# Spreading token weights by transfers from DRAM, and adding the causal mask inside the row maxima, in a two-layer hybrid kernel

## The chip, the cores and the metric

The kernel runs on one core of a Trainium2 chip, in one launch. Its time is the device time of that core in microseconds (us): the median of three runs before the change is 1032.24 us (1031.15 to 1035.77). A profile is one further execution with the hardware's profiler on; its times are set against its own total. The engines are PE (TensorE, products), DVE (VectorE), ACT (ScalarE), POOL (GpSimd) and SP (SyncE), which here only issues transfers.

## What is computed

The input `x` is 4 sequences of 512 tokens with 128 channels. Six blocks follow, each added to `x`; the first two matter here. The first is causal softmax attention with 16 heads of 8 channels, computed blockwise with a running row maximum:

```python
scores = scale * jnp.einsum('bhtd,bhsd->bhts', Q, kb)
future = kv_pos[None, :] > q_pos[:, None]
scores = jnp.where(future[None, None], -jnp.inf, scores)
m_new = jnp.maximum(m, jnp.max(scores, axis=-1, keepdims=True))
```

The second is a mixture of 8 experts, two per token, and it is used twice (behind the softmax attention and behind the FAVOR attention). A token enters an expert multiplied by its routing weight:

```python
scores = jax.nn.softmax(logits.astype(jnp.float32), axis=-1)
top_vals, idx = jax.lax.top_k(scores, K)
xs = xt[:, None, :] * weights[:, :, None]
for e in range(E):
    mask = (idx == e).astype(x.dtype)
    h = jax.nn.silu(jnp.einsum('tkd,hd->tkh', xs, w1[e]) + b1[e])
    x2 = jnp.einsum('tkh,dh->tkd', h, w2[e]) + b2[e]
    x3 = jnp.einsum('tkd,hd->tkh', xs, w3[e]) + b3[e]
    y = y + jnp.sum(x2 * x3 * mask[:, :, None], axis=1)
z = jax.nn.silu(xt @ sw1.T) * (xt @ sw2.T) @ sw3.T
```

FAVOR attention, a gated linear attention, two quantized feed-forward blocks and a retention block make up the rest.

## The kernel before

**Stages.** `x` stays in SBUF as `X`. The work is done per sequence (512 tokens). `attention` (L409) goes first, as a software pipeline of 96 steps plus a tail of 8 steps and more; PE's order is written out there, the other engines' order is left to the framework. After it everything from the experts to the end is emitted by one planner, `Clock.steps` (L178). Each stage is a generator that names what it needs; the planner keeps its own estimate of when each engine is free, and of all that could go next it emits what could start first, with a priority `far` (the table `FAR`, L39) between equals. The numbers in `clock.later("dve", 0.7, ...)` and `clock.pe(0.34)` are those estimates in us. PE, ACT, DVE and POOL then run exactly in the order in which the planner emitted; SP's order is left to the framework.

**Attention's maxima.** Step n works on a group of four heads, a part of the query chunks and two of the heads. `maxima` (L464) makes the scores of a query chunk of 128 rows against all keys up to its diagonal (128, 256, 384 or 512 columns) in a bank of PSUM. The diagonal block must be masked: `late` (L475) adds a matrix of 0 and -1e30 with one product per chunk and head, identity `identb` times `lateb`, both in bf16, into the same bank (256 products in all). `keep` (L480) then takes the row maximum with `tensor_reduce` on DVE (L484) straight from the bank into a column of `tops`. Eight steps later `weights` (L496) forms the exponentials: ACT reads the bank (L509), POOL sets the future to zero (L511). All banks come from one set of eight, so a bank that DVE or ACT has not read yet keeps PE waiting.

**Experts.** There are 8 rounds q (4 sequences, twice) of 8 experts. `route` (L659) finds the weights of the two chosen experts per token (DVE, then POOL), in `parts` (L692) written as three bf16 parts whose sum is exact (`split`, L627: three casts and two subtractions on POOL). `by_expert` (L701) transposes them on PE to `wT`, one row per expert and part. `scaled` (L720) spreads one expert's row over all 128 channels with a product of `wT` with a selecting matrix `sel` (24 rows, bf16) into a bank, and DVE multiplies the bank with the tokens `xnT` into `xe` (L725):

```python
ps = bank()
self.mm(ps, k["sel"][:, e * P:(e + 1) * P], wT[q][:3 * E])
xe = self.new(more["sm"], [P, T], "xe")
return xe, lambda: tt(xe, xnT[q], ps, ALU.mult)
```

`first` (L727) multiplies `xe` with w1 and w3 (two f32 products, each recorded as two instructions of 512 columns), ACT applies tanh and biases (L735, L737), DVE finishes the silu (L736: `h` and `g`, both in SBUF); `second` (L739) multiplies with w2 and forms `y`, on DVE from the bank (L746) or, for odd experts of rounds 0 to 4, on ACT and POOL (L747, L748); POOL adds `y` to the sum (L749). `total` (L751) adds the shared expert, a term for tokens that did not choose an expert (`c8` times the other rows of `wT`) and the sum into a bank, and DVE adds it to `X`. The generator `moe` (L1154) runs them in a pipeline: `spread` two experts ahead of `first`, `second` two behind it.

**Transfers.** SP's queue loads the inputs at the start, further weights when attention frees their room, stores `X` in DRAM once per sequence as `kept` (L1208), and stores the output at the end (L1687).

Of the kernel before, what the change touches and what calls it, by code (L numbers as in the profile page):

```python
# [10 lines left out]
F32 = mybir.dt.float32  # L11
BF16 = mybir.dt.np(mybir.dt.bfloat16)
U32 = mybir.dt.uint32
# [17 lines left out]
UP = 1.0 + 2.0 ** -22  # L31
EXP, TANH, SILU = ("exp",), ("exp", "silu"), ("silu",)
EARLY = 2

# [4 lines left out]
FAR = {  # L39
    "moe": (34,),  # L40
    "shared": (589, 230, 101, 186, 338, 444, 196, 385),
    "total": (34, 334, 167, 440, 467, 482, 19, 193),
    "in": (0, 0, 100, 527, 450, 482, 45, 323),
    "inward": (364, 104, 384, 461),
    "favor": (378, 171, 133, 588),
    "gates": (135, 468, 451, 231),
    "keys": (237, 481, 541, 82),
    "gated": (377, 269, 540, 166),
    "first": (55, 466, 547, 542),
    "retention": (54, 134, 224, 459),  # L50
    "leveled": (326, 293, 76, 394),
    "second": (75, 76, 343, 438),
}
# [3 lines left out]
def _constants():  # L57
    f = np.float32
    c = {}
    c["ident"] = np.eye(P, dtype=f)  # L60
    r = np.arange(P)
    g, d = r // 32, r % 32
    of = d[:, None] // DH == np.arange(NG)[None, :]
    row = d[:, None] == DH * ((np.arange(NG) + 1) % NG)[None, :]
    c["rows"] = np.concatenate([of, row, of | row], axis=1)
    c["heads"] = r[:, None] // DH == np.arange(H)[None, :]
    c["own"] = np.tile(r[:, None] % 32 // DH == r[None, :] // M, (1, 2))
    c["first"] = np.tile(np.arange(E, 0, -1, dtype=f), (P, 1))
    c["two"] = (r[:, None] // DI == np.arange(2)[None, :]).astype(f)
    lev = np.zeros((P, 6, 64), f)  # L70
    for l in range(6):
        right = r[(r >> l) & 1 == 1]
        lev[:, l, :] = ((r[:, None] >> (l + 1)) == (right[None, :] >> (l + 1))) & ((r[:, None] >> l) & 1 == 0)
    c["lev"] = lev.reshape(P, -1)
    c["tri"] = r[:, None] <= r[None, :]

    lo, hi = f(np.log(1.0 - 0.999)), f(np.log(1.0 - 0.9))
    gam = (f(1.0) - np.exp(np.linspace(lo, hi, H, dtype=f)).astype(f)).astype(np.float64)
    hd, mid = gam[r // DH], r - P // 2
    c["qdec"] = hd[:, None] ** mid[None, :]  # L80
    c["kdec"] = hd[:, None] ** -mid[None, :]
    c["cdec"] = hd[:, None] ** P
    of = r[:, None] // DH == r[None, :] // DH
    c["same"] = of * c["cdec"]
    c["group"] = (d[:, None] // DH == np.arange(NG)[None, :])
    c["avg"] = of / DH
    c = {k: np.ascontiguousarray(v.astype(f)) for k, v in c.items()}

    c["lateb"] = np.where(r[None, :] > r[:, None], f(-1e30), f(0)).astype(BF16)

    c["sel"] = np.repeat(np.arange(3 * E)[:, None] % E == np.arange(E)[None, :], P, axis=1).astype(BF16)
    c["identb"] = np.eye(P, dtype=f).astype(BF16)
    return c
# [142 lines left out]
class Net:  # L236
# [172 lines left out]
    def attention(self, beside=None, ended=None):  # L409
# [12 lines left out]
        with ExitStack() as ctx:  # L422
# [3 lines left out]
            tops = [self.new(big, [P, J, P], f"tops{G}") for G in range(NG)]  # L426
            vs = [self.new(big, [P, J, H, 32], f"vpad{i}") for i in range(2)]
            for t in tops:
                nc.vector.memset(t, 0.0)
# [34 lines left out]
            def maxima(g, s, h):  # L464
# [6 lines left out]
                def score(i, n):  # L471
                    c, o = step[n]
                    self.mm(ps[i][:, o:o + (c + 1) * P], q[strips[i], chunks[c]], kk[strips[i], :(c + 1) * P], start=(n == 0), stop=False)

                def late():  # L475
                    for i in heads:
                        for n, (c, o) in enumerate(step):
                            self.mm(ps[i][:, o + c * P:o + (c + 1) * P], k["identb"], k["lateb"], start=False, stop=(n == len(step) - 1))

                def keep():  # L480
                    r = 8 * ((G + 1) % NG)
                    for i in heads:
                        for c, o in step:
                            nc.vector.tensor_reduce(top[:, c, 32 * i + r:32 * i + r + 1], ps[i][:, o:o + (c + 1) * P], AX.X, ALU.max)  # L484

                return [[lambda i=i, n=n: score(i, n) for n in range(len(step))] for i in heads], late, keep

# [8 lines left out]
            def weights(g, s, h):  # L496
# [16 lines left out]

                return [[lambda i=i, n=n: score(i, n) for n in range(len(step))] for i in heads], lambda: None, keep

# [58 lines left out]
            with self.tc.manual_schedule(engines={mybir.EngineType.PE}):  # L574
# [4 lines left out]
                while n < max(at):  # L579
# [7 lines left out]
                    for i in range(2):  # L587
                        for strip in range(2):
                            for todo, _, _ in now:
                                if i < len(todo[strip]):  # L590
                                    todo[strip][i]()
                    for _, late, _ in now:
                        late()
                    for _, _, keep in now:
                        keep()
# [6 lines left out]

    def experts(self, ctx):
        nc, k = self.nc, self.k
# [8 lines left out]
        def enlarge(ctx):  # L613

            for name, bufs in (("mid", 2), ("sm", 4)):
                more[name] = ctx.enter_context(self.tc.tile_pool(name="e_" + name, bufs=bufs))
# [4 lines left out]
        half, half3, twice2 = (self.new(big, [P, E], n) for n in ("half", "half3", "twice2"))  # L621
        bf16 = mybir.dt.bfloat16
        W8 = 32 + 3 * E
        c8 = big.tile([W8, P], bf16, tag="c8", name=self.nm("c8"))
        xn, xnT, wT, shares, sums, part = ({} for _ in range(6))

        def split(to, x):  # L627

            for i in range(3):
                nc.gpsimd.tensor_copy(to[..., i, :], x)  # L630
                if i < 2:
                    nc.gpsimd.tensor_tensor(x, x, to[..., i, :], ALU.subtract)

        def of_none():
# [11 lines left out]
            stt(none, none, -1.0, b3, ALU.mult, ALU.mult)  # L646
            parts = big.tile([P, W8], bf16, tag="c8p", name=self.nm("c8p"))
            nc.gpsimd.memset(parts[:, :32], 0.0)
            split(parts[:, 32:].rearrange("p (k e) -> p k e", e=E), none)
            ps = bank([W8, P], bf16)  # L650
            nc.tensor.transpose(ps, parts, k["identb"])
            nc.scalar.copy(c8, ps)
# [6 lines left out]
        def route(q):  # L659
# [32 lines left out]
            def parts():  # L692
                nc.gpsimd.tensor_tensor(s, s, c, ALU.mult)
                w = part[q] = rt.tile([P, J, W8], bf16, tag="part", name=self.nm("part"))
                v = w.rearrange("p j (k e) -> p j k e", e=E)
                nc.vector.tensor_scalar(v[:, :, 3:], c.unsqueeze(2).to_broadcast([P, J, 4, E]), -1.0, 1.0, ALU.mult, ALU.add)
                split(v, s)

            return less, lambda: nc.scalar.activation(s, s, AF.Exp), shared_out, again, parts

        def by_expert(q):  # L701

            ps = bank([W8, T], bf16)
            for j in range(J):
                nc.tensor.transpose(ps[:, chunks[j]], part[q][:, j], k["identb"])
            wT[q] = pre.tile([W8, T], bf16, tag="wT", name=self.nm("wT"))
            return lambda: nc.scalar.copy(wT[q], ps)

# [11 lines left out]
        def scaled(q, e):  # L720

            ps = bank()
            self.mm(ps, k["sel"][:, e * P:(e + 1) * P], wT[q][:3 * E])
            xe = self.new(more["sm"], [P, T], "xe")
            return xe, lambda: tt(xe, xnT[q], ps, ALU.mult)  # L725

# [177 lines left out]
    def front(self, out):  # L904
# [5 lines left out]
        with ExitStack() as ctx, ExitStack() as now, self.tc.tile_pool(name="kept", bufs=1, space=bass.MemoryType.DRAM) as dram:  # L910

            rooms = ("identb", "ws", "first", "we", "sel")
            self.room(tp(now, "w", 1), rooms)
            ex = self.experts(now)
            with ExitStack() as att:
                self.load(tp(att, "wa", 1), ("wa", "rows", "lateb"))
                right = tp(att, "qw", 1, side="right")
# [175 lines left out]
            with ExitStack() as over, self.banks():  # L1093
# [29 lines left out]
                def routed(q):  # L1123
# [16 lines left out]
                    yield [op, when("y", q - 3) if q > 2 else 0.0], "bank"  # L1140
                    known["in", q] = later("act", 0.6, pe(0.5), ex.by_expert(q), "bank")
                    yield known["in", q]
# [11 lines left out]
                def moe():  # L1154
# [4 lines left out]
                    def spread(n):  # L1159
                        q, e = all_[n]  # L1160
                        yield [when("in", q)], "bank"
                        x, do = ex.scaled(q, e)
                        xe[n] = x, later("dve", 0.7, pe(0.34), do, "bank")
                        if e == E - 1:
                            known["left", q] = clock.since

# [10 lines left out]

                    for n in range(-2, len(all_) + 2):
                        if n + 2 < len(all_):
                            yield from spread(n + 2)  # L1180
                        if 0 <= n < len(all_):
# [671 lines left out]
```

## Time and profile before

| What | Value |
|---|---|
| median of 3 runs | 1032.24 us |
| profiled execution, total | 1032.06 us |
| its span, first to last instruction | 1030.3 us |
| mean granted clock of PE | 0.94 |
| ACT, busy | 560.0 us (54%) |
| transfers, whole span | 9.82 MB, 10 GB/s |
| attention ends (its last addition to X) | about 243 us |
| last product of the experts | 643 us |

A row of a group reads: line, engine, operation, output and inputs by the program's names, partitions x elements, count, then busy time and mean ns of one, then the idle time of that engine ahead of them and what ended it. Almost every product has line 400, a helper, so products are told apart by their tiles. Products overlap, so what one costs PE is read from the timeline, from its start to the start of the next, and not from its own duration.

### The profile page before, as it was taken

To read this page: it belongs to the slowest core of one execution; us is meant where nothing else is said; L and a number is where in the kernel's file an instruction comes from. 1 tells how busy PE (TensorE), PEld (TensorE's weight loads), DVE (VectorE), ACT (ScalarE), POOL (GpSimd) and SP (SyncE) were. 2 spreads that over 40 slices of the span, in tenths; PEclk is the share of its full clock that TensorE was granted. 3 is DMA by queue.
4 is the path that set the end of the run, shared out by engine and by line. 5 is a ranking of instruction groups with operands and counts; after the bars stand their busy time and mean duration, and the time that the engine had idled before them with its cause. 6 is when DMAs were issued, how large, how long until landed. Compare 5 with 4: busy or idle time off the path is not lost.

```text
span 1030.3 us, 17949 instructions
## 1 busy us (share of the span) xinstructions
PE 890.4 (86%) x6624; PEld 541.1 (53%) x6624; DVE 734.2 (71%) x1808; ACT 560.0 (54%) x1076; POOL 448.3 (44%) x899
## 2 busy tenths in 40 slices
PE   5999999998999989998988989678798977778734
PEld 3545555554335555444534457446687765566523
DVE  5657777755776898978877755596685864977664
ACT  3556656564774665757476742384345555465422
POOL 2434544341674554555556424463224515343322
PEclk9989999999999999999999999898998997997867
DMA  4000001000000000000000000100000000000000
GB/s 158 2 2 2 2 16 41 2 1 22 0 1 1 1 1 1 2 0 2 11 1 11 1 1 11 32 1 1 1 1 2 1 1 2 1 12 1 12 10 14
DMA packets 8387, 9.82 MB, mean 10 GB/s; under 512 B 1740, under 2 KB 6860, under 8 KB 8036
## 3 DMA queue, kind: packets, MB, share of 16 engines
q1 hardware_dynamic: 8292, 8.60, 2.6%
q8 instruction: 54, 0.88, 0.3%
q14 instruction: 41, 0.34, 0.1%
HBM read 6.50 MB, written 2.10 MB: 8 GB/s over the span
## 4 chain that ended last, share of the span: by engine, by line
PE 53%; DVE 27%; POOL 8%; ACT 7%; issue 4%; DMA 1%; SPq 0%; DVEq 0%; ACTq 0%; POOLq 0%
PE bank L400 48%; DVE D L1015 2%; DVE arg L831 2%; PE bank L382 2%; DVE top L828 1%; DVE h L736 1%; DVE bn L330 1%; DVE D L1606 1%; DVE D L1605 1%; PE bank L1655 1%; DVE top L829 1%; POOL rnt L310 1%; PE bank L492 1%; POOL rstdbe1t L310 1%; DVE den L887 1%
## 5 line engine op out<-in xcount | busy, mean ns | idle before, releaser
L484 DVE TENSOR_REDUCE tops<-bank 128x1 f32<-128x128 f32 (+3 forms) x256 | 110.1, 485 | 55.3 <-PE bank L400 55.2
L400 PE MATMUL bank<-xe,we 128*128 128x512 f32 x256 | 127.6, 620 | 4.5 <-ACT x L737 2.9
L509 ACT ACTIVATE w<-bank 128x512 f32<-128x512 f32 (+1 forms) x192 | 90.5, 526 | 69.5 <-PE bank L400 65.8
L511 POOL TENSOR_SCALAR_AFFINE_SELECT w<-w 128x128 f32<-128x128 f32 x256 | 70.3, 297 | 116.6 <-ACT w L509 116.1
L400 PE MATMUL bank<-qm,kz 32*128 32x384 f32 (+3 forms) x512 | 101.9, 471 | 1.1 <-DVE tops L484 0.6
L400 PE MATMUL bank<-kz,q 32*128 32x512 f32 (+3 forms) x512 | 98.2, 476 | 0.0
L749 POOL TENSOR_TENSOR sum<-sum,y 128x512 f32<-128x512 f32 x56 | 76.7, 1369 | 43.9 <-DVE y L746 41.6
L736 DVE SCALAR_TENSOR_TENSOR h<-h,g 128x512 f32<-128x512 f32 x64 | 60.2, 941 | 21.2 <-ACT g L735 21.1
L400 PEld LDWEIGHTS bank<-xe,we 128*128 128x128 f32 x256 | 43.6, 190 | 49.2 <-issue 29.7
L400 PE MATMUL bank<-h,we 128*128 128x512 f32 x128 | 67.4, 610 | 2.1 <-DVE arg L831 2.1
L735 ACT ACTIVATE h<-bank,half 128x512 f32<-128x512 f32 x64 | 43.8, 684 | 31.6 <-PE bank L400 31.3
L403 DVE TENSOR_TENSOR X<-X,bank 128x512 f32<-128x512 f32 x32 | 21.9, 685 | 50.8 <-PE bank L400 33.0
L400 PE MATMUL bank<-xs,wg 128*128 128x512 f32 x96 | 52.9, 657 | 5.0 <-DVE R L1308 3.3
L400 PEld LDWEIGHTS bank<-kz,q 32*128 32x128 f32 x512 | 38.2, 189 | 32.1 <-issue 11.6
L400 PEld LDWEIGHTS bank<-qm,kz 32*128 32x128 f32 x512 | 47.4, 185 | 13.1 <-DVE tops L484 2.3
L400 PE MATMUL bank<-w,vpad 128*32 128x256 f32 (+3 forms) x512 | 49.0, 449 | 1.8 <-DVE ru L675 1.1
L725 DVE TENSOR_TENSOR xe<-xnT,bank 128x512 f32<-128x512 f32 x64 | 43.2, 678 | 9.9 <-PE bank L400 9.9
L1741 POOL TENSOR_SCALAR_AFFINE_SELECT rw<-rw 128x1024 f32<-128x1024 f32 x32 | 35.4, 1122 | 31.8 <-ACT rw L1740 31.8
L737 ACT ACTIVATE x<-bank,half 128x512 f32<-128x512 f32 x64 | 44.0, 688 | 0.0
L735 ACT ACTIVATE g<-bank,ws 128x512 f32<-128x512 f32 x64 | 43.7, 682 | 0.0
L1740 ACT COPY rw<-bank 128x512 f32<-128x512 f32 x64 | 32.9, 596 | 14.4 <-PE bank L400 14.3
L382 PE MATMUL bank<-ident,xn 128*128 128x128 f32 x80 | 17.5, 314 | 24.9 <-ACT xn L342 19.0
(426 smaller groups left out, 2163.2 us busy)
## 6 DMA issues: line engine op xcount, KB each, us to landing
we<-in_we_dram SPq DMA_DIRECT2D x1, 1536.0 KB, 6.9
wg<-in_wg_dram SPq DMA_DIRECT2D x1, 1280.0 KB, 6.1
X<-in_x_dram SPq DMA_DIRECT2D x4, 256.0 KB, 4.4
kept<-X SPq DMA_DIRECT2D x4, 256.0 KB, 2.5
out_dram<-X SPq DMA_DIRECT2D x4, 256.0 KB, 2.3
wf<-in_wf_dram SPq DMA_DIRECT2D x1, 560.0 KB, 7.5
ws<-in_ws_dram SPq DMA_DIRECT2D x1, 400.0 KB, 4.6
wb<-in_wb_dram SPq DMA_DIRECT2D x1, 320.0 KB, 2.9
```

The source lines that it names most:

```text
L382: self.nc.tensor.transpose(ps[:, j * P:(j + 1) * P], xn[:, j, :], self.ident)
L400: self.nc.tensor.matmul(out, lhsT=lhsT, rhs=rhs, start=start, stop=stop)
L484: nc.vector.tensor_reduce(top[:, c, 32 * i + r:32 * i + r + 1], ps[i][:, o:o + (c + 1) * P], AX.X, ALU.max)
L509: nc.scalar.activation(w[:, :end], ps[i][:, :end], AF.Exp, scale=scale)
L511: nc.gpsimd.affine_select(out=w[:, o:o + P], in_=w[:, o:o + P], pattern=[[1, P]], compare_op=ALU.is_ge, fill=0.0, base=0, channel_multipli ...
L725: return xe, lambda: tt(xe, xnT[q], ps, ALU.mult)
L735: return (h, x3, lambda: (act(h, ph, AF.Tanh, scale=0.5, bias=half[:, e:e + 1]), act(g, ph, AF.Identity, bias=b1[:, e:e + 1])), lambda: st ...
L736: lambda: stt(h, h, 1.0, g, ALU.add, ALU.mult),
L737: lambda: act(x3, p3, AF.Identity, scale=0.5, bias=half3[:, e:e + 1]))
L749: lambda: nc.gpsimd.tensor_tensor(sums[q], sums[q], y, ALU.add))
L1740: ops = [later("act", 0.6, t, lambda n=n, i=i: nc.scalar.copy(w[n][:, i, :], pp[2 * n + i]), "bank") for i in range(2)]
L1741: ended.append(later("pool", 1.15, ops, lambda flat=flat: nc.gpsimd.affine_select(out=flat, in_=flat, pattern=[[0, 2 * J], [1, P]], compar ...
```

## The change

1. **Mask.** `late` and its 256 products go, with `lateb` and `identb`. A constant `late` of 128 x 512 in f32 takes their place: zeros, and the triangle of -1e30 in the last 128 columns. `keep` uses one fused DVE operation that adds the last `e` columns of `late` (SBUF) to the scores (bank), writes the sum to a scratch tile `junk` and the maximum to the column of `tops`.
2. **Token weights.** The three bf16 parts and `sel` go; the weights stay f32 (one part of 8 columns). `by_expert` copies the transposed rows to SBUF and then stores 8 rows of 512 in DRAM (`rows_of[q]`). `scaled` reads one row back to all 128 partitions by a transfer (SP) into `xe`, out of five buffers of its own (two ahead and three more), and multiplies it in place with `xnT`: on DVE for odd experts, on POOL for even ones. It takes no bank. `c8`, the transposes and the products with them become f32.
3. **Planner.** The rows of a round count as ready 5.5 us after the copy; the scaling counts as 0.85 us on DVE or 1.4 us on POOL, 0.5 us after it is emitted. A round counts as left when its last scaling has been done, not when it is emitted. All priorities in `FAR` have other values.

```diff
-    "moe": (34,),
-    "shared": (589, 230, 101, 186, 338, 444, 196, 385),
-    "total": (34, 334, 167, 440, 467, 482, 19, 193),
+    "moe": (80,),
+    "shared": (394, 388, 591, 530, 598, 130, 157, 493),
+    "total": (127, 37, 531, 99, 92, 3, 562, 529),
...
+    late = np.zeros((P, T), f)
+    late[:, T - P:] = np.where(r[None, :] > r[:, None], f(-1e30), f(0))
...
-                def late():
-                    for i in heads:
-                        for n, (c, o) in enumerate(step):
-                            self.mm(ps[i][:, o + c * P:o + (c + 1) * P], k["identb"], k["lateb"], start=False, stop=(n == len(step) - 1))
...
-                            nc.vector.tensor_reduce(top[:, c, 32 * i + r:32 * i + r + 1], ps[i][:, o:o + (c + 1) * P], AX.X, ALU.max)
+                            e = (c + 1) * P
+                            nc.vector.tensor_tensor_reduce(
+                                out=junk[:, :e], in0=ps[i][:, o:o + e], in1=k["late"][:, T - e:], scale=1.0, scalar=-3e38,
+                                op0=ALU.add, op1=ALU.max, accum_out=top[:, c, 32 * i + r:32 * i + r + 1])
...
+            for name, bufs in (("mid", 2), ("sm", 4), ("xe", AHEAD + 3)):
...
+                nc.gpsimd.tensor_tensor(v[:, :, 0], s, c, ALU.mult)
+                nc.vector.tensor_scalar(v[:, :, 1:], c.unsqueeze(2).to_broadcast([P, J, 4, E]), -1.0, 1.0, ALU.mult, ALU.add)
...
+            def keep():
+                nc.scalar.copy(wT[q], ps)
+                nc.sync.dma_start(rows_of[q], wT[q][:E])
...
-            ps = bank()
-            self.mm(ps, k["sel"][:, e * P:(e + 1) * P], wT[q][:3 * E])
-            xe = self.new(more["sm"], [P, T], "xe")
-            return xe, lambda: tt(xe, xnT[q], ps, ALU.mult)
+            xe = self.new(more["xe"], [P, T], "xe")
+            nc.sync.dma_start(xe, rows_of[q][e, :].partition_broadcast(P))
+            return xe, lambda eng: eng.tensor_tensor(xe, xnT[q], xe, ALU.mult)
...
-                    known["in", q] = later("act", 0.6, pe(0.5), ex.by_expert(q), "bank")
+                    op = later("act", 0.6, pe(0.5), ex.by_expert(q), "bank")
+                    known["in", q] = later(f"rows{q}", 5.5, op)
...
-                        xe[n] = x, later("dve", 0.7, pe(0.34), do, "bank")
+                        if e % 2:
+                            xe[n] = x, later("dve", 0.85, clock.since + 0.5, lambda: do(nc.vector))
+                        else:
+                            xe[n] = x, later("pool", 1.4, clock.since + 0.5, lambda: do(nc.gpsimd))
                         if e == E - 1:
-                            known["left", q] = clock.since
+                            known["left", q] = xe[n][1]
```

## The prediction

> **What bounds the kernel now.** I read the page's engine rows first, then busy time by stretch, the chain of waits, the costliest groups, and PE's timeline where the change cuts.
>
> ```profile
> PE 890.4 (86%) x6624; PEld 541.1 (53%) x6624; DVE 734.2 (71%) x1808; ACT 560.0 (54%) x1076; POOL 448.3 (44%) x899
> 25.00:225.00 200.00, 195.64 (x1906) 103.12 (x1904) 142.26 (x393) 118.03 (x244) 84.69 (x319) 0.98 0.03 9
> 243.00:312.00 69.00, 68.71 (x186) 28.42 (x187) 51.98 (x103) 45.29 (x78) 39.21 (x48) 1.00 0.03 8
> 312.00:602.00 290.00, 264.92 (x1463) 137.31 (x1462) 228.76 (x469) 182.35 (x322) 151.59 (x285) 0.99 0.01 3
> 645.00:1030.00 385.00, 289.01 (x2546) 224.16 (x2545) 267.54 (x704) 183.08 (x371) 144.88 (x174) 0.86 0.02 6
> PE 53%; DVE 27%; POOL 8%; ACT 7%; issue 4%; DMA 1%; SPq 0%; DVEq 0%; ACTq 0%; POOLq 0%
> ```
>
> The first line is the page's, the next four are busy time by stretch (start:end, length, then PE, PEld, DVE, ACT, POOL, granted clock, DMA share, GB/s), the last is the chain. Attention fills the first stretch, the experts alone the second, the experts beside FAVOR and the first gates the third, gates, retention and FFN the last. PE is 98%, 100% and 91% busy in the three that the change touches and 75% in the one that it does not. So work taken off PE in the first three can show. In attention DVE is second, at 71%.
>
> **Part 1: the mask.** The 256 mask products go; the 256 reductions become reductions of a sum with a second operand.
>
> ```profile
> L400 PE MATMUL bank<-lateb,identb 128*128 128x128 bf16 x256 | 31.4, 226 | 0.0
> L484 DVE TENSOR_REDUCE tops<-bank 128x1 f32<-128x512 f32 x64 | 41.1, 685 | 7.7 <-PE bank L400 7.7
> L494 DVE SCALAR_TENSOR_TENSOR qm<-q,rows,bank 128x512 f32<-128x512 f32 x16 | 11.9, 743 | 1.0 <-PE bank L492 1.0
> L1015 DVE TENSOR_TENSOR_SCAN D<-run,D 128x512 f32<-128x512 f32 x16 | 20.5, 1338 | 1.4 <-ACT D L1010 1.4
> L725 DVE TENSOR_TENSOR xe<-xnT,bank 128x512 f32<-128x512 f32 x64 | 43.2, 678 | 9.9 <-PE bank L400 9.9
> 137.59 0.28 PE L400 MATMUL bank<-lateb,identb 128*128 128x128 bf16 x2
> 137.81 0.64 PE L400 MATMUL bank<-w,vpad 128*32 128x256 f32 x8
> ```
>
> Products overlap, so their 226 ns is no price. The timeline gives it: two start at 137.59 and the next work at 137.81. Over all of attention the median is 0.21 us for the 64 pairs (0.12 to 0.22) and 0.32 for the 32 fours (0.23 to 0.33): 64 x 0.19 + 32 x 0.29 in the mean = **21.5 us of PE**. In the chain between 25 and 245 us PE's lines hold some 86% (products 76.5%, the transposes of L492, L535, L382 and L1535 another 9%), so 18.5 us of it should be felt.
>
> The new DVE operation is not in this trace. From below: a plain sum with one operand in a bank and one in SBUF takes 678 ns, the reduction 685, so it may cost nothing more, and I see no reason for less since as many elements stream. From above: the scan, the only row that carries a result from element to element beside a second operand, takes 1338, that is 0.65 more for 512 elements and 0.41 for the mean width of 320. The nearest row is the three-operand operation out of a bank, 743: +0.06 us each. Then DVE has 142.3 + 243 x 0.06 = 157 us of work in a stretch that PE would leave at 200 - 20 = 180: 87%. That still lies beside PE, but it hands back banks later, for which PE already waits 10.3 us here (13 times, on the maxima), so I charge 2.5 us. The product's end no longer stands between the scores and the maxima, which helps and is in the 18.5. Part 1: **-16 us**, ends -21.5 and +42 (below). The scratch output that all 256 share is written by one engine in order and adds no wait across engines.
>
> The accumulator deserves a sentence of its own. The Trainium skill, "VectorE: DVE Perf Modes", section "Two Vector instructions with no wait between them", has it that an operation that also writes out its accumulator is two instructions, the main one and a read of the accumulator; no instruction here does that, so no run here shows it.
>
> **Part 2: the token weights.** 64 products (L723) go, 64 transfers of 256 KB come, and the scaling of even experts moves to POOL.
>
> ```profile
> 283.74 0.39 PE L400 MATMUL bank<-wT,sel 24*128 24x512 bf16 x1
> 284.06 1.98 PE L400 MATMUL bank<-xe,we 128*128 128x512 f32 x4
> L736 DVE SCALAR_TENSOR_TENSOR h<-h,g x64: 666/692/1747, 257.4 to 625.1; 128x512 f32<-128x512 f32 x64
> L725 DVE TENSOR_TENSOR xe<-xnT,bank x64: 671/678/689, 251.4 to 594.0; 128x512 f32<-128x512 f32 x64
> L749 POOL TENSOR_TENSOR sum<-sum,y 128x512 f32<-128x512 f32 x56 | 76.7, 1369 | 43.9 <-DVE y L746 41.6
> kept<-X SPq DMA_DIRECT2D x4, 256.0 KB, 2.5
> ```
>
> - **PE.** One product holds PE for 0.32 us (283.74 to 284.06), 64 of them 20 us: 22 in the second stretch, 42 in the third. Products and transposes that turn from bf16 to f32 give some back: 32 of `total`'s at 0.08 become like its f32 neighbours (0.12), 32 transposes go from 0.085 to 0.12, together +2.4. The second stretch is paid in full (22 x 0.31 = 6.9). Of the third's 13.1 I count 45%, PE's product share of the chain there (43.5%): 5.9. Net -10.4.
> - **DVE** loses 64 x 0.68 = 43 us and gets 32 operations with both operands in SBUF. The rows show what that means: with an operand in a bank the time is 671 to 689 ns, with both in SBUF (L736) 666 to 1747, mean 941, the long ones lying beside a POOL operation. 32 x 0.94 = 30, so DVE is 13 us lighter, less some 6 if L736 gets 0.1 longer beside a busier POOL.
> - **POOL** gets 32 x 1.37 = 44 and loses 24 casts (7.4) and 16 subtractions (4.6). In the second stretch: 39 + 10 x 1.37 - 3 = 50 of about 63 us, 79%. In steady state an expert of the first five rounds now has two POOL operations, 2.74 us, against PE's 3.09 - 0.31 = 2.78. It stays under, barely; that is the first thing to fail.
> - **Transfers.** 256 KB landed 2.3 to 4.4 us after issue; 16.8 MB over 350 us are 48 GB/s, where the first slice moved 158. Five buffers let a transfer start when the product three experts earlier has read its buffer, about 8 us ahead of need, so 2.5 to 4.4 us are covered by PE's own work; without that cover 64 x 2.5 us would be exposed. SP issues 0.45 us each, in one queue with the stores of `kept`: a store that waits would hold up what stands behind it. The two-hop way through DRAM (2.5 + 2.5 us, eight times) is ahead of need by a round, and in the first two rounds falls inside attention. The very first transfer needs room that attention frees around 242; the shared products cover 243 to 250, so I charge nothing, at most 3 us.
>
> Part 2: **-10 us**, ends -18 (all of PE's time) and +10 (POOL late in the first rounds, SP's queue blocked a few times).
>
> **Part 3: the order.** All priorities are new, so the planner emits another order from 243 us on. In the last stretch no work changes, and I see in the trace no reason for a sign. Its longest single waits (PE for POOL's L1612: 10.3 and 7.5 us) set the size: one such wait more or less, **0, within 12 us**.
>
> **Sum.** The profiled execution took 1032.06 us (span 1030.3), 0.2 below the median of 1032.24. 1032.1 - 16 - 10 = **1006 us**.
>
> **Rivals.**
> 1. *All of it is felt and the order is kind*: -21.5 - 17.7, up to 10 more from the order: 984 to 994. For it: PE has hardly a gap in two stretches. Against: in the third stretch DVE and ACT end many waits. 0.13.
> 2. *DVE becomes attention's bound.* If each maximum costs a small second instruction (the nearest, a reduction of 32 elements, has 187 ns) on top of 0.06, DVE has 142.3 + 243 x 0.25 = 203 us in what is now 200. Attention then gains nothing (+3), the experts keep -10: 1018 to 1028, middle 1025. By the page named above this is what would happen. 0.12.
> 3. *Slower: the fused maximum runs at the scan's rate.* 142.3 + 243 x 0.41 = 242 us for 200: +42 - 10 = 1064 (1048 to 1075). It decides from about 0.28 us more per maximum, where 142.3 + 243 x 0.28 = 210 eats both gains. For it: the scan is the only kin in the trace that carries a value. Against: the plain reductions carry a running maximum at 685 ns. 0.08.
> 4. *The gain is given back*: POOL or SP's queue late in the experts (+10 where I have -10) or a worse order at the end (+12): 1028 to 1044. 0.17.
> 5. *The forecast*, 994 to 1018: 0.50.
>
> About 0.5% (5 us) is what a measurement of this kernel can tell from no change. Faster by more: 0.50 + 0.13 + 0.10 of rival 2 = 0.73; within: 0.02 of rival 2 and 0.05 of rival 4 = 0.07; slower: 0.12 of rival 4 and 0.08 of rival 3 = 0.20. The range 985 to 1042 leaves out rival 3 and the edges.
>
> **What would show it.** Right: attention ends near 225 instead of 241, its DVE row for 512 elements stands at 0.69 to 0.80 us, PE stays above 95% there; the pure expert stretch runs at 2.8 us per expert. Wrong: a DVE row of 0.95 us or more, or a second small row beside it, with PE waiting for the maxima; POOL above 90% with products waiting for `xe`; transfers that land later than 5 us after issue; a last part (now 387 us, from the end of the experts at 643 to the end) that changes by more than 12 us.

## The result and the profile after

| Kernel | median us | runs | ratio to before, 95% |
|---|---|---|---|
| before (same chip) | 1031.70 | 4 | |
| after | 1019.11 (1017.53 to 1020.30) | 4 | 0.9876 [0.9860, 0.9892] |

The change makes the kernel 12.6 us faster, where the forecast was 26 and its range 985 to 1042. The profiled execution took 1018.07 us (span 1016.1). These lines answer to the ones of before: the engine row and the chain from the page, then busy time by stretch (the last one ends with the kernel at 1016; the experts still run in its first 22 us).

```profile
PE 871.8 (86%) x6336; PEld 542.2 (53%) x6336; DVE 750.2 (74%) x2032; ACT 558.2 (55%) x1076; POOL 490.0 (48%) x887
...
PE 49%; DVE 30%; POOL 10%; ACT 6%; issue 5%; DMA 0%; SPq 0%; DVEq 0%; ACTq 0%; POOLq 0%
```

```profile
25.00:225.00 200.00, 192.64 (x1683) 97.03 (x1683) 156.84 (x637) 120.00 (x250) 85.25 (x322) 0.95 0.03 9
243.00:312.00 69.00, 62.22 (x183) 29.64 (x183) 49.68 (x102) 43.93 (x78) 50.75 (x60) 0.95 0.26 80
312.00:602.00 290.00, 250.54 (x1363) 143.88 (x1362) 212.07 (x414) 165.84 (x297) 164.47 (x249) 0.90 0.13 39
645.00:1016.00 371.00, 295.15 (x2726) 229.54 (x2724) 280.21 (x726) 186.79 (x380) 153.40 (x179) 0.90 0.02 6
```

Two columns tell the story. PE has less to do, but in the second and third stretch it is no longer full (62 of 69 us where it was 68.7; 250.5 of 290 where it was 264.9), and its **granted clock** (the share of full speed that it was given), 0.98, 1.00 and 0.99 before, is 0.95, 0.95 and 0.90. DVE's busy time in attention is 156.8 against 142.3, the 157 that the forecast had. Attention (to the start of its last addition to X) ends at 238.1 instead of 242.3; the rest takes 778.0 instead of 788.0 us.

A sum over stretches of 5 us splits each span in three: PE's work as it would be at full clock, what the clock took (busy time x (1 - granted clock), an estimate, since the ends of products are modelled), and PE's idle time.

| Kernel | span | work | clock | idle |
|---|---|---|---|---|
| before | 1030.3 | 847 | 43 | 140 |
| after | 1016.1 | 810 | 62 | 144 |

The change took 37 us of work off PE, about what the forecast counted (21.5 + 20 - 2.4 = 39). 19 came back as a lower clock and 4 as waiting. The sum is good to some 10 us only: it gives 843 for the run with the new order alone (below), whose instructions are those of before, and 11 and 21 us less than before for two runs that leave out the same 256 products. These totals hide that the kernel's parts moved in opposite ways. The same sum by part (the experts' part goes to their last product, at 643 before and 667 after):

| Part | length, before and after | work | clock | idle |
|---|---|---|---|---|
| attention | 242.3, 238.1 | 222, 207 | 3, 11 | 17, 20 |
| experts' part | 400.9, 429.3 | 371, 353 | 3, 28 | 27, 48 |
| last part | 387.1, 348.7 | 254, 249 | 37, 23 | 96, 76 |

In the experts' part, where the token weights changed, 18 us of work went and 46 of clock and idle time came; the last part, whose code did not change, is 38 us shorter. The experiments ask where the waits come from, and what the new table does by itself.

### The profile page after: what moved, and what is told of

It reads as the page before. It is cut to its first block, busy times and chain, and to the rows that moved or that the text cites. A ratio compares the mean times of both kernels' runs of the same rounds, so it can differ in the third digit from the quotient of the medians.

```text
span 1016.1 us, 17875 instructions
## 1 busy us (share of the span) xinstructions
PE 871.8 (86%) x6336; PEld 542.2 (53%) x6336; DVE 750.2 (74%) x2032; ACT 558.2 (55%) x1076; POOL 490.0 (48%) x887
## 4 chain that ended last, share of the span: by engine, by line
PE 49%; DVE 30%; POOL 10%; ACT 6%; issue 5%; DMA 0%; SPq 0%; DVEq 0%; ACTq 0%; POOLq 0%
PE bank L399 44%; DVE junk L480 2%; PE bank L381 2%; DVE h L728 2%; DVE D L1007 2%; DVE bn L329 1%; DVE D L1602 1%; DVE den L879 1%; POOL sum L741 1%; DVE D L1601 1%; POOL D L1608 1%; POOL xe L717 1%; PE bank L490 1%; PE bank L533 1%; DVE X L402 1%
## 5 line engine op out<-in xcount | busy, mean ns | idle before, releaser
L480 DVE CUSTOM_DVE_ANT_0 junk<-bank,late 128x128 f32<-128x128 f32 (+3 forms) x256 | 125.2, 489 | 41.1 <-PE bank L399 20.2
L399 PE MATMUL bank<-xe,we 128*128 128x512 f32 x256 | 134.2, 651 | 13.6 <-POOL xe L717 11.6
L399 PE MATMUL bank<-qm,kz 32*128 32x256 f32 (+3 forms) x512 | 109.7, 484 | 0.8 <-DVE tops L480 0.7
L399 PE MATMUL bank<-kz,q 32*128 32x512 f32 (+3 forms) x512 | 104.8, 494 | 1.2 <-ACT kz L462 0.6
L399 PEld LDWEIGHTS bank<-xe,we 128*128 128x128 f32 x256 | 50.8, 208 | 74.6 <-issue 47.0
L399 PE MATMUL bank<-h,we 128*128 128x512 f32 x128 | 71.3, 642 | 2.4 <-DVE KD L1043 1.2
L399 PEld LDWEIGHTS bank<-kz,q 32*128 32x128 f32 x512 | 43.1, 196 | 36.6 <-DVE tops L480 15.3
L399 PEld LDWEIGHTS bank<-qm,kz 32*128 32x128 f32 x512 | 51.1, 190 | 16.6 <-DVE tops L480 7.0
L717 POOL TENSOR_TENSOR xe<-xnT,xe 128x512 f32<-128x512 f32 x32 | 46.2, 1446 | 13.4 <-DMA xe<-rows 12.8
L1651 PE MATMUL bank<-ident,D 128*128 128x128 f32 (+1 forms) x96 | 17.0, 315 | 25.7 <-POOL D L1608 25.0
```

What stands on the lines that cost most here:

```text
L399: self.nc.tensor.matmul(out, lhsT=lhsT, rhs=rhs, start=start, stop=stop)
L480: nc.vector.tensor_tensor_reduce(out=junk[:, :e], in0=ps[i][:, o:o + e], in1=k["late"][:, T - e:], scale=1.0, scalar=-3e38, op0=ALU.add, o ...
L717: return xe, lambda eng: eng.tensor_tensor(xe, xnT[q], xe, ALU.mult)
```

## Experiments

Ratios are to the kernel before, on the same chip as each run; its medians there were 1031.6 to 1032.4. "Attention ends" is the start of its last addition to X in the trace.

### The order alone

`c_order` is the kernel before with nothing but the new `FAR`:

```diff
-    "moe": (34,),
+    "moe": (80,),
...
```

> The kernel before with the new table of priorities alone. Theory D: the 10 us that the change gains behind attention come from work taken off PE, and priorities chosen for other work help nothing here: 1027 to 1045. Rival E: they come from the order: 1017 to 1024.

1008.79 us (1007.84 to 1013.45), 0.9778 [0.9745, 0.9811]: **23.6 us faster, more than the whole change.** By the three-part sum its span of 1006.5 is 843 work, 46 clock, 118 idle: the gain is idle time of PE, 22 us. All but 2.6 us of the gain lie behind attention, which ends at 239.7. To see whether some rows carry it, the table was split, and two tables were drawn at random (every number from 0 to 600):

> The kernel before with the new table's four rows of the experts (moe, shared, total, in) and the old nine rows of the later stages. Theory A (the table's 23 us come from the experts' own rows): 1008 to 1014. Theory B (no row carries it; the whole sequence does): anything between 1005 and 1045, and the two halves' differences do not add up to 23 us.

> The complement: the new table's nine rows of the later stages, the old four rows of the experts. Theory A: 1026 to 1032. Theory B: anything between 1005 and 1045, and the sum of the two halves differs from 23 us by more than 8.

> The kernel before with a table of due times drawn at random, each number from 0 to 600. Theory A (orders scatter on both sides of the old table, so the new one is one of many): within 20 us of 1032 on either side. Theory B (both tables are better than a chance one, the new one more so): slower than 1036.

> A second table drawn in the same way. Theory A: within 20 us of 1032 on either side, and at least one of the two draws at or below 1032. Theory B: slower than 1036, as the first.

| Table | median us | ratio, 95% |
|---|---|---|
| new rows of the experts, old others | 1044.63 | 1.0128 [1.0052, 1.0203] |
| new rows of the later stages, old others | 1016.89 | 0.9854 [0.9812, 0.9895] |
| drawn 1 | 1092.69 | 1.0599 [1.0573, 1.0625] |
| drawn 2 | 1102.97 | 1.0695 [1.0675, 1.0715] |

The halves give +12.2 and -15.5, in sum -3 where the whole gives -23.6, so the totals do not add. By part the traces show what they do:

| Table | attention | experts' part | last part |
|---|---|---|---|
| old (before) | 242.3 | 400.9 | 387.1 |
| new rows of the experts, old others | 240.8 | 417.0 | 380.6 |
| new rows of the later stages, old others | 239.1 | 422.1 | 351.2 |
| new (`c_order`) | 239.7 | 416.9 | 349.8 |

The new rows of the later stages shorten the last part by 36 of its 37 us by themselves. Its work on PE stays near 250 us; 22 us of idle time go, and 10 us of what the clock took. Either half makes the experts' part 16 to 21 us longer, and both together 16: there the clock takes 17 us in `c_order` where it took 3. The other runs confirm it, the two drawn tables apart: the last part is 349 to 351 us long in all that have the new rows of the later stages, and 381 to 388 in all that have the old ones. Which of these rows it is remains open. The random tables cost 60 and 71 us. So an order is worth up to 94 us here, the old and the new table are both far from these two draws, and a size of "one such wait more or less", 12 us, was the wrong measure.

### The mask

`a_mask_only` is the kernel before with the mask's edits alone; `a_no_mask` takes the 256 products out and puts nothing in their place:

```diff
-                def late():
-                    for i in heads:
-                        for n, (c, o) in enumerate(step):
-                            self.mm(ps[i][:, o + c * P:o + (c + 1) * P], k["identb"], k["lateb"], start=False, stop=(n == len(step) - 1))
...
```

> The kernel before with part 1 alone (fused maxima, no mask products; weights, planner and order as before). Theory A: each maximum now holds DVE about 0.2 us longer from start to start (an accumulator read of 0.08 us and the gaps around it), 47 us in all, so attention is bounded by DVE and PE in turn and gains 4 us: last addition of attention at 238, total about 1028. Rival B: the maxima are no bound, attention's lost gain comes from something that part 2 does during attention; then attention gains 16 to 20 here and the total is 1012 to 1016.

> The kernel before without any masking of the maxima: no mask products, the plain reduction as before. The row maximum then also sees later keys of the diagonal block; it is only the shift of the softmax, so the output changes by rounding alone. Theory A: with PE's products gone and DVE's maxima as cheap as before, attention gains most of 21.5: 15 to 20 us, total 1012 to 1017. Rival C: the products were covered anyway and their going is worth about what the change got, 4 us: total about 1028.

| Kernel | median us | ratio, 95% | attention ends |
|---|---|---|---|
| `a_mask_only` | 1029.65 | 0.9977 [0.9958, 0.9996] | 238.5 |
| `a_no_mask` | 1019.85 | 0.9875 [0.9850, 0.9899] | 229.5 |

Even a mask that costs nothing is worth 12.8 us of attention, not 18.5; and of those the fused maximum kept 3.8 in attention and 2.7 in the whole. The timeline of DVE shows why. First plain reductions of before (x2 means two in a row, 1.29 us together), then the fused operation of after:

```profile
32.85 1.28 DVE L484 TENSOR_REDUCE tops<-bank 128x1 f32<-128x512 f32 x2
...
153.27 1.01 DVE L484 TENSOR_REDUCE tops<-bank 128x1 f32<-128x384 f32 x2
```

```profile
24.01 0.69 DVE L480 CUSTOM_DVE_ANT_0 junk<-bank,late 128x512 f32<-128x512 f32 x1
24.63 0.08 DVE L480 DVE_READ_ACCUMULATOR2_ANT tops<- 128x1 f32 x1
24.86 0.69 DVE L480 CUSTOM_DVE_ANT_0 junk<-bank,late 128x512 f32<-128x512 f32 x1
25.47 0.08 DVE L480 DVE_READ_ACCUMULATOR2_ANT tops<- 128x1 f32 x1
25.70 0.69 DVE L480 CUSTOM_DVE_ANT_0 junk<-bank,late 128x512 f32<-128x512 f32 x1
```

The main operation costs what the reduction did (0.69). But two plain reductions of 0.68 take 1.28 together, so the second starts 0.60 after the first; the fused ones start 0.84 apart, because a second instruction, the read of the accumulator, stands between them. That is 0.24 more per maximum of 512, and 0.25 per one of 384 (0.71 in the trace of after against 1.01 - 0.55). A row's mean duration hides both: the overlap of plain reductions and the gap of fused ones. The Trainium skill, "VectorE: DVE Perf Modes", section "Two Vector instructions with no wait between them", names an accumulator output two instructions; this trace agrees, 82 ns for the second and 256 of them. The waits of PE's weight loads for the maxima rise from 10.3 us (13 times) to 24.3 (48 times).

Two runs put a small instruction behind plain reductions, to test that price by itself.

```diff
                             nc.vector.tensor_reduce(top[:, c, 32 * i + r:32 * i + r + 1], ps[i][:, o:o + (c + 1) * P], AX.X, ALU.max)
+                            nc.vector.tensor_scalar(small, self.onesp, 1.0, None, ALU.mult)
```

> The mask left out of the maxima (as before: later keys of the diagonal block are seen, so only the softmax's shift differs), plain reductions, no mask products, but one small VectorE instruction of 128x1 behind each of the 256 reductions. Theory A (the second small instruction of the fused maximum is what keeps the gain away): attention ends at 236 to 240 us instead of 229.5, the whole 1025 to 1030. Theory B (the loss is in the wide addition of the fused instruction or in the clock alone): as without the small instruction, 1019 to 1021, attention ending at 229 to 231.

1042.09 us, 1.0101 [1.0083, 1.0118], attention ending at 251.7: beyond both theories. The trace says why: the small instructions wait for nothing, and the framework moved them forward, six to ten in a row between two maxima near 31 and 80 us. All 22 us are lost by the fifth of the 16 groups and nothing behind it. The run does not price a second instruction in its place. `a_no_mask_behind` ties it there:

```diff
+                            nc.vector.tensor_scalar(top[:, c, 32 * i + r:32 * i + r + 1], top[:, c, 32 * i + r:32 * i + r + 1], 1.0, None, ALU.mult)
```

> The mask left out of the maxima (only the softmax's shift differs), plain reductions, and behind each of the 256 reductions one VectorE instruction of 128x1 that multiplies the maximum just written by 1, so that it can't move ahead. Theory A (a second small instruction per maximum is what keeps the fused maximum's gain away): attention ends at 236 to 242 us instead of 229.5, the whole 1026 to 1033. Theory B (the fused instruction's width or the clock alone): attention ends at 229 to 231, the whole 1019 to 1021.

```profile
66.21 0.68 DVE L479 TENSOR_REDUCE tops<-bank 128x1 f32<-128x512 f32 x1
66.92 0.15 DVE L480 TENSOR_SCALAR tops<-tops 128x1 f32<-128x1 f32 x1
66.99 0.68 DVE L479 TENSOR_REDUCE tops<-bank 128x1 f32<-128x512 f32 x1
```

1023.93 us (1020.58 to 1032.41), 0.9907 [0.9877, 0.9936], attention ending at 233.7 (the profiled execution is its slowest, span 1030.6; behind attention it is 8 us longer than `a_no_mask`). Between the theories: start to start is now 0.78, and attention loses 4.2 us against `a_no_mask`, where the fused form (`a_mask_only`) loses 9.0. The order is that of theory A, but by the 512 columns alone the second instruction (0.18 more) should cost nearly as much as the fused form (0.24 more). The narrower maxima explain why it doesn't. Medians from the start of one maximum to that of the next, in us:

| Columns | plain | plain and a second instruction | fused |
|---|---|---|---|
| 128 | 0.20 | 0.26 | 0.33 |
| 256 | 0.33 | 0.39 | 0.58 |
| 384 | 0.47 | 0.66 | 0.71 |
| 512 | 0.60 | 0.79 | 0.84 |

With 64 maxima of each width that is an estimated 32 us more of DVE for the second instruction and 55 for the fused form, 58% of it, and attention's loss is 47%. So the loss roughly goes with DVE's time from start to start, and the instruction put behind was the cheaper one. How the fused form's own share divides between the read itself and the gaps around it is not settled.

### The token weights

`d_transfer_pool` and `d_transfer_dve` put the transfers into `c_order` without a change of the planner's numbers, so that the order of emission stays; the first scales even experts on GpSimd, the second all on VectorE. The two `d_old_...` are the same with the old table. `b_weights_neworder` is after with its mask edits undone.

```diff
-            ps = bank()
-            self.mm(ps, k["sel"][:, e * P:(e + 1) * P], wT[q][:3 * E])
-            xe = self.new(more["sm"], [P, T], "xe")
-            return xe, lambda: tt(xe, xnT[q], ps, ALU.mult)
+            xe = self.new(more["xe"], [P, T], "xe")
+            nc.sync.dma_start(xe, rows_of[q][e, :].partition_broadcast(P))
+            return xe, lambda: (nc.vector if e % 2 else nc.gpsimd).tensor_tensor(xe, xnT[q], xe, ALU.mult)
```

> The changed kernel with the mask products back and the plain reduction (part 1 undone; transfers, scaling on POOL and the new order kept). Theory A: part 1 is worth 4 us and the parts add up: 1023. If part 1 gives later stages something too (DVE or the clock), 1026 or more; if it is worth nothing, 1019.

> Part 2 alone at a fixed order: the new table of priorities, mask products kept, and the planner still counting a product and a scaling on DVE for each expert, so that every engine gets its work in the same order as in the run with the new table alone (1008.8); in fact the token weights come by transfer and even experts are scaled on POOL. Theory F: transfers and POOL are what cost the 15 us between 1008.8 and 1023.6, whatever the planner believes: 1019 to 1030. Rival G: the 15 us come from the order that the planner makes when it is told of POOL and transfers; then PE's 20 us show here: 990 to 1003.

> The same with all scaling on DVE. Theory F with POOL as the culprit: the transfers alone are harmless and PE's 18 us show in part, 992 to 1004. Theory F with the transfers as the culprit: no better than the run with POOL, 1019 to 1030.

> Part 2 alone at the old order (the old table, planner unaware, mask products kept; against 1032). Theory F: slower than before, 1040 to 1050, as at the new order. Rival G, and the forecast on record: 1012 to 1024.

> The kernel before, its old table and its planner's costs, token weights by transfers and all 64 scalings on VectorE. With half of them on GpSimd this took 1045.0 us. Theory A (GpSimd's half is the loss, the exchange of products for transfers is worth 0 to 6 us): 1026 to 1035. Theory B (the transfers themselves come too late at this order): 1040 to 1046.

| Table | planner's costs | scaling | median us | ratio, 95% | against products, same table |
|---|---|---|---|---|---|
| new | of after | half GpSimd (`b_weights_neworder`) | 1023.61 | 0.9910 [0.9887, 0.9932] | +14.8 |
| new | of before | half GpSimd | 1018.68 | 0.9876 [0.9849, 0.9902] | +9.9 |
| new | of before | VectorE | 1008.66 | 0.9760 [0.9718, 0.9802] | -0.1 |
| old | of before | half GpSimd | 1044.95 | 1.0128 [1.0094, 1.0162] | +12.9 |
| old | of before | VectorE | 1052.84 | 1.0188 [1.0155, 1.0221] | +20.4 |

In no pairing do the transfers gain. The second row is the median of five executions from 1011.5 to 1019.9, and its profiled one is the fastest, so its trace understates the loss. My theory after the first four rows, that GpSimd's half is the loss, falls with the fifth: at the old table VectorE alone is the slower one. In the experts' part PE's account is the same kind in every trace: against the same table with products 18 to 20 us of work go, and idle time (13 to 26 us) and the clock (up to 23) take them back. Late transfers are not the cause: half of them landed within 3.1 us in the trace of after, and behind the first scaling of each trace none waits more than 0.71 us for one. What is left is the scaling: it takes longer, and what it costs seems to depend on where the order puts it, which no run tests alone. The groups show what is slower, of after and then of `d_old_transfer_dve`:

```profile
L717 POOL TENSOR_TENSOR xe<-xnT,xe 128x512 f32<-128x512 f32 x32 | 46.2, 1446 | 13.4 <-DMA xe<-rows 12.8
...
L717 DVE TENSOR_TENSOR xe<-xnT,xe 128x512 f32<-128x512 f32 x32 | 31.1, 972 | 0.0
```

```profile
L722 DVE TENSOR_TENSOR xe<-xnT,xe 128x512 f32<-128x512 f32 x64 | 63.8, 1007 | 0.0
```

Over all traces with transfers one scaling with both operands in SBUF takes 914 to 1068 ns on DVE in the mean and 1417 to 1495 on POOL, against 678 out of the bank: all on DVE, 58 and 64 us instead of 43. How one late scaling is paid twice is seen in after at 357 us. POOL's timeline, then PE's, then PE in stretches of 1 us (busy times, then the clock):

```profile
354.29 1.26 POOL L741 TENSOR_TENSOR sum<-sum,y 128x512 f32<-128x512 f32 x1
355.51 1.72 POOL L740 TENSOR_TENSOR y<-y,x 128x512 f32<-128x512 f32 x1
357.31 1.70 POOL L741 TENSOR_TENSOR sum<-sum,y 128x512 f32<-128x512 f32 x1
358.96 1.26 POOL L717 TENSOR_TENSOR xe<-xnT,xe 128x512 f32<-128x512 f32 x1
```

```profile
353.56 1.88 PE L399 MATMUL bank<-xe,we 128*128 128x512 f32 x4
...
356.23 1.02 PE L399 MATMUL bank<-h,we 128*128 128x512 f32 x2
360.28 3.78 PE L399 MATMUL bank<-xe,we 128*128 128x512 f32 x4 [3.03 <-POOL xe L717]
```

```profile
358.00:359.00 1.00, 0.00 (x0) 0.00 (x0) 0.90 (x6) 1.00 (x3) 1.00 (x2) 1.00 0.01 2
359.00:360.00 1.00, 0.00 (x0) 0.00 (x0) 0.93 (x4) 1.00 (x3) 1.00 (x2) 0.65 0.00 0
...
361.00:362.00 1.00, 1.00 (x2) 0.34 (x1) 0.25 (x1) 0.00 (x0) 0.75 (x4) 0.50 0.00 0
...
365.00:366.00 1.00, 1.00 (x2) 0.39 (x2) 0.11 (x1) 0.00 (x0) 0.92 (x2) 0.50 0.47 166
```

The scaling stood on POOL behind two sums and the product for `y`, 4.7 us of work without a gap, and PE waited 3.03 us. Then the clock is 0.50 until 366, and the same two products (four instructions) take 3.78 us instead of 1.88: one wait of 3 us cost some 6. Over 312 to 602 us the clock took 0.10 x 250.5 = 25 us in after and 0.01 x 264.9 = 3 before. Not all of that comes from the transfers: with the new table alone (`c_order`, the line below) it took 0.06 x 263.7 = 16 us.

```profile
312.00:602.00 290.00, 263.70 (x1409) 136.53 (x1408) 221.05 (x446) 176.02 (x311) 147.87 (x260) 0.94 0.01 3
```

Last, what the products cost at all, in `c_order`: `d_unscaled_product` keeps them but drops the scaling, `d_unscaled` drops both. Their output leaves out the token weights.

```diff
             ps = bank()
             self.mm(ps, k["sel"][:, e * P:(e + 1) * P], wT[q][:3 * E])
-            xe = self.new(more["sm"], [P, T], "xe")
-            return xe, lambda: tt(xe, xnT[q], ps, ALU.mult)
+            return xnT[q], lambda: None
```

> The kernel before with the new table of due times, in which the 64 selecting products still run on TensorE (0.34 us each) but nothing reads them: VectorE's 64 scalings are left out, and the experts take the unscaled tokens (the token weights are left out of the result). Against the table alone (1008.8 us) it takes away 64 DVE instructions of 0.68 us, 43 us of DVE. If VectorE sets the pace of the experts' stretch: about 990. If TensorE does: 1004 to 1009.

> As the run with the products left in, but without the 64 products too (token weights left out of the result). My step of the prediction counted them at 20 us of TensorE that were felt. Theory A (the products are felt, and the loss of the change's scaling ate them): 15 to 20 us below the run that keeps the products. Theory B (the products fill time in which TensorE waits anyway, or are given back by its clock): within 5 us of that run.

998.32 us, 0.9676 [0.9658, 0.9693], and 991.97, 0.9609 [0.9589, 0.9629]. The products' 20 us of PE are worth **6.3**, the 43 us of VectorE's scaling 10.5. That falls between the theories, nearer to B: two thirds of PE's time in the products fills time in which PE would wait or be slowed. Token weights at no cost at all would gain 17 us, and the transfers bring more scaling time, not less.

### Together

`e_order_mask` is the new table with the mask's edits and the products; `e_order_nomask` the new table without the mask.

> The kernel before with the new table and part 1, token weights by products as before. If the parts add up: 1008.8 - 3 to 4.5 = 1004 to 1006, faster than both kernels.

> The new table of due times together with the maxima without the mask (the shift of the softmax alone differs, the weights do not), token weights by products as before. If the two gains add (table 23.6 us, mask left out 12.5 us): about 996. If the table's gain comes from the same idle time as attention's: 1004 to 1008.

1007.21 us (1005.78 to 1011.88), 0.9775 [0.9741, 0.9809], and 999.39 (996.05 to 1000.70), 0.9677 [0.9654, 0.9701]. The mask's edits are worth 1.6 us at the new table, within what can be told. Leaving the mask out of the maxima adds 9.4 of its 12.5 to the table's gain. `c_order`, `d_transfer_dve`, `e_order_mask` and `e_order_nomask` beat both kernels; the last shifts the softmax by a maximum that includes up to 127 later keys, so it would lose small weights where a later key scores far higher.

## Why the prediction was wrong

- **Part 1, forecast -16, measured -1.6 to -4.5** (1032.4 to 1029.65 alone; 1008.8 to 1007.2; 1023.6 to 1019.1). PE's saving was counted rightly (by the three-part sum the run without the mask has 21 us less work on PE). The step that failed is the price of "+0.06 us each": with the accumulator's read it is 0.24 from start to start at 256 to 512 columns and 0.13 at 128, rival 2's mechanism near rival 2's price (0.25). DVE's busy time came out at the forecast 157 us all the same, because busy time leaves out the gap behind the read (0.15 us in the lines above). That rival was given 0.12 although the page of the Trainium skill that it rests on says just this; the rows were read as durations, and the trace of before already held the start to start of 0.60. Its range, 1018 to 1028, holds the result, but by luck: it counted the experts' -10, which did not come, and nothing for the order. A second step failed as well: 18.5 of 21.5 felt. With a free mask 12.8 are felt.
- **Part 2, forecast -10, measured 0 to +20, +12 in after itself** (1019.1 against 1007.2). The mean of a scaling was right (0.94 on DVE forecast, 0.97 measured; 1.37 and 1.45 on POOL), and so were the transfers (half landed within 3.1 us, the slowest in 5.3). What failed is the step that PE's 20 us are felt at 6.9 + 5.9: at the new table, where it was measured, their ceiling is 6.3. And that POOL with two operations per expert "stays under, barely" held in the mean (POOL 74% busy in the second stretch) but not in the order: three long operations in a row stood ahead of a scaling. No step had a price for PE's clock.
- **Part 3, forecast 0 within 12, measured -23.6 alone.** "I see in the trace no reason for a sign" was taken for "no size". The failed step is that the last part was priced at one wait of 12 us: with about the same work (254 and 249 us of PE) it is 37 us shorter, and the experts' part, which had no price for the order, is 16 longer. Alone, with the mask's edits, and under the transfers (half on POOL, all on VectorE) the new table is worth 23.6, 22.4, 26.3 and 44.2 us.
- **The sum.** -23.6 for the order, +14.8 for the weights, -4.5 for the mask, each on top of the one before, give -13.3; the result is -12.6. The sign came out right, and the time fell into the range, by luck: through the part that was put at nothing. One range was added up wrongly as well: rival 4 (+10 for the experts instead of -10, or +12 at the end) gives 1026, 1018 or with both 1038, not 1028 to 1044.
- **The signs to watch** did their work: attention ended at 238 and not 225 (from 242.3 by the same measure, where the forecast has 241), a second small row stood beside the maximum, products waited for `xe` on POOL (11.6 us of PE's waits in the experts' stretch), and the last part changed by more than 12 us (349 us instead of 387, with the experts ending 24 us later).
- **Open**: which of the later stages' rows shorten the last part, and through which wait; why VectorE alone is the worse at the old table (by the sum the clock takes 26 us of its experts' part, against 15 with half on GpSimd); whether a table made for the transfers would turn them into a gain. The whole change under the old table was not tried.

## What to carry to other kernels

When a planner's priorities change together with the code, run the priorities alone and the code alone first, and compare stage by stage: here the order's gain lay in a part whose code did not change, and the total hid a loss beside it. Price an operation by start to start in the timeline, not by its mean row, and look whether it ends in a second instruction. An engine that is 95% busy doesn't give back all the time that is taken off it: measure the ceiling with a kernel that leaves the work out, and look at the granted clock behind PE's waits, since a wait can cost about twice its length (some 6 us for one of 3.03 here).

## What the runs showed of the hardware

- The granted clock fell to 0.50 some 2 us into a wait of 3.03 us and stayed there 6.8 us, over which products took twice as long. The Trainium skill, "TensorE: Matmul & The Clock Gate", section "What's actually happening", puts the fall behind an idle window of about 3.4 us; here a shorter wait was enough.
- That is no exception. The clock falls 25 times in the trace of after and 20 times in that of before (apart from the end), and ahead of 17 and 15 of these falls no wait of PE that reaches into the last 3.4 us was as long as 3 us. Each low stretch has a clock of 0.50 and lasts 3.4, 6.8, 10.2 or 13.7 us, whole multiples of 3.41. Every wait of 3 us or more that began at full clock (8 and 5) had a fall in it or within 3.4 us behind it.
- Two plain reductions of 0.68 us out of a bank follow each other after 0.60 us; with a small instruction of 0.15 between them after 0.78; a fused sum and maximum of 0.69 follows the one before after 0.84.
- The read of an accumulator is a recorded instruction of 82 ns on DVE.
- Each of the two instructions of an f32 product with 512 columns from SBUF to a bank took 0.47 us at full clock and 0.95 at the lower one (1.88 and 3.78 for four).
